# Layer 3 of a four-layer graph network: inverse sums kept on 32 partitions per head and spread by ScalarE copies, block sums in another pool, converted adjacency in a pool of its own

## The chip, the cores and the metric

The kernel runs on one core of one Trainium2 chip. TensorE (PE) multiplies matrices into PSUM, VectorE (DVE), ScalarE (ACT) and GpSimd (POOL) work element by element, and transfers are queued by SyncE (SP), ScalarE and GpSimd. The metric is the device time of one execution in microseconds; lower is better.

## The reference

A graph of 3,327 nodes with 256 features each, and a 3,327 x 3,327 adjacency. Four layers follow each other, each of them `x = layernorm(x + attention(x, adj))`. Layers 0 to 2 have one attention head. Layer 3 is two passes of a four-head attention (64 features per head), of which the first is what the change touches:

```python
h = jnp.einsum('nf,hfd->hnd', x, W)
f1 = jnp.einsum('hnd,hd->hn', h, a[:, :D])
f2 = jnp.einsum('hnd,hd->hn', h, a[:, D:])
e = jax.nn.leaky_relu(f1[:, :, None] + f2[:, None, :], ALPHA)
e = jnp.where(adj[None, :, :] > 0, e, NEG)
att = jax.nn.softmax(e, axis=-1)
out = jax.nn.elu(jnp.einsum('hnm,hmd->hnd', att, h))
```

The second pass takes the first one's output (nodes by 4 x 64 features) as its input, with other weights, and its result is added to x and normalised.

## The kernel before, in words

Nodes are cut into 26 tiles of 128 (the last has 127), and the tiles into four blocks of 7, 7, 6 and 6 (`blocks`, `sizes`), so a block has 896 or 768 columns. Layer 0 works with lists of neighbours and gathers (`sparse0`, L904, L924, L930, L1004, L1007) and takes the first half of the time. Layers 1 and 2 (`one_head`, L1688) and the two passes of layer 3, called l3a and l3b (`many_heads`, L1732), are dense: for each block b of target nodes they run over all 26 source tiles j.

In `many_heads`, one step j loads a tile of the adjacency as bf16 (`adjacent`, L1626; layer 1 loads it as int32, converts it on ScalarE and stores it for the later layers, L1635 to L1639). VectorE then makes four tiles of weights, one per head (`weigh`, L1614): `e = max(rate, q) * at`, in which the exponentials of the scores have been factored, so that no exponential is taken per edge. TensorE multiplies them in two column halves (`parts`): 16 matmuls of 32 feature columns (L1751) and 8 that sum the weights, each sum repeated on 32 partitions (L1759), so that partitions 32h to 32h+31 of `accs[x][pairs]` all hold the sum of head h. The accumulators fill six PSUM banks; two are left for everything else (`misc((6, 7))`).

At a block's end ScalarE copies the features (L1773, into `o`, features by nodes) and the sums (L1775, into `sums`) out of PSUM. What remains to be done with the block is a generator (`finish_hidden` for l3a, `finish_last` for l3b), appended to `pending`. `work_off` takes one step of it behind j = 0 and behind each j from 4 on of the next block (L1765), so that its instructions come into the engines' queues between those of the steps j. On PE, DVE and ACT the order is the program's (`manual_schedule`, L2004); on SP and POOL a scheduler sets it.

`finish_hidden` before: seven (or six) matmuls turn the sums to nodes by heads (`inverses`, L1794), VectorE takes the reciprocal of 28 or 24 numbers per partition (L1800), and then units of two node tiles go through the stages of `staged`: `spread` (eight matmuls with a broadcast inverse against the identity bring each head's inverses to its 64 feature partitions, L1833, and ScalarE copies them from PSUM, L1841), three steps later `scale` (VectorE multiplies `o`, L1846; ScalarE makes the exponential part of elu, L1810, L1811), then `elu` (L1852) and `project` (matmuls L1548 with the next pass's weights, and seven small ScalarE instructions per tile, L1557 to L1575). `staged` emits later stages first within a step. At the end the block's exponentials go through HBM to all partitions (`send_rates`, `load_rates`, L1594 to L1612).

Tiles of one tag in a pool share a fixed number of buffers. Tag "e" of the pool `edges` has 8: the weights, the int32 adjacency of layer 1, and the `sums` of layer 3. Tag "at" has 3. Tag "spread" of the pool `work` has 4.

Of the kernel before, what the change touches and what calls it, by code (L numbers as in the profile page):

```python
# [8 lines left out]
F32 = mybir.dt.float32  # L9
BF16 = mybir.dt.bfloat16  # L10
# [9 lines left out]
P = 128  # L20
BANK = 512
# [29 lines left out]
def gat_stack(  # L51
# [29 lines left out]
    nc = tc.nc  # L81
# [3 lines left out]
    heads = l3_w1.shape[0]  # L85
    hd = l3_w1.shape[2]
    assert dim == kc * P and heads * hd == dim

    def rows_of(it):
        return min(P, n - it * P)  # L90
# [4 lines left out]
    small = ctx.enter_context(tc.tile_pool(name="small", bufs=4))  # L95
# [124 lines left out]
    wide = max(sizes) * P  # L220
    banks_n = [(lo, min(n, lo + BANK)) for lo in range(0, n, BANK)]

    def cols_of(block):
        return block[0] * P, min(n, (block[-1] + 1) * P)
# [1273 lines left out]
    def layers(rs, early=0, rest=None):  # L1498


        head_p = rs.enter_context(tc.tile_pool(name="head_p", bufs=1))
        edges = rs.enter_context(tc.tile_pool(name="edges", bufs=3))
        work = rs.enter_context(tc.tile_pool(name="work", bufs=2))
        feats = rs.enter_context(tc.tile_pool(name="feats", bufs=1))
        rates = rs.enter_context(tc.tile_pool(name="rates", bufs=1))
# [10 lines left out]
        def misc(banks):  # L1516
            spare[0] += 1
            i = banks[spare[0] % len(banks)]
            return ps.tile([P, BANK], F32, tag=f"b{i}", name="misc")
# [106 lines left out]
        def adjacent(j, b, first=False):  # L1626

            pn = rows_of(j)
            c0, c1 = cols_of(blocks[b])
            w = c1 - c0  # L1630
            at = edges.tile([P, wide], BF16, tag="at", name="at")
            if not first:
                copy_rows(nc.sync, at[:pn, :w], at_d[j * P : j * P + pn, c0:c1])
                return at
            at_i = edges.tile([P, wide], I32, tag="e", name="at_i", bufs=8)  # L1635
            copy_rows(nc.sync, at_i[:pn, :w], adj_t[j * P : j * P + pn, c0:c1])
            nc.scalar.copy(at[:pn, :w], at_i[:pn, :w])  # L1637
            copy_rows(nc.scalar, at_d[j * P : j * P + pn, c0:c1], at[:pn, :w])
            return at_i  # L1639
# [92 lines left out]
        def many_heads(layer, nxt, finish):  # L1732

            pairs = layer.nh // 2
            for b, block in enumerate(blocks):
                c0, c1 = cols_of(block)
                half = (len(block) + 1) // 2 * P
                parts = [(0, half), (half, c1 - c0)]
                work_until(lambda: layer.rate[b] is not None)
                accs = [[bank(3 * x + y) for y in range(pairs + 1)] for x in range(len(parts))]  # L1740
                for j in range(nt):
                    pj = rows_of(j)
                    work_until(lambda: layer.feat[j] is not None)
                    at = adjacent(j, b)
                    es = [layer.weigh(j, b, at, h_of) for h_of in range(layer.nh)]
                    f = layer.feat[j]
                    for x, (lo, hi) in enumerate(parts):

                        for at0 in range(0, dim, 32):
                            p, q = divmod(at0, 2 * hd)  # L1750
                            nc.tensor.matmul(  # L1751
                                accs[x][p][q : q + 32, : hi - lo],
                                f[:pj, at0 : at0 + 32],
                                es[at0 // hd][:pj, lo:hi],
                                start=(j == 0), stop=(j == nt - 1),
                            )
                    for x, (lo, hi) in enumerate(parts):
                        for h_of in range(layer.nh):
                            nc.tensor.matmul(  # L1759
                                accs[x][pairs][h_of * 32 : (h_of + 1) * 32, : hi - lo],  # L1760
                                f[:pj, dim + h_of : dim + h_of + 1].to_broadcast([pj, 32]),
                                es[h_of][:pj, lo:hi],
                                start=(j == 0), stop=(j == nt - 1),
                            )
                    if j == 0 or j >= LATER:  # L1765
                        work_off()
                work_until(lambda: not pending)

                o = turn_p.tile([P, pairs, wide], F32, tag="ht", name="o")
                sums = edges.tile([P, wide], F32, tag="e", name="sums", bufs=8)  # L1770
                for x, (lo, hi) in enumerate(parts):
                    for p in range(pairs):
                        nc.scalar.copy(o[:, p, lo:hi], accs[x][p][:, : hi - lo])  # L1773
                for x, (lo, hi) in enumerate(parts):
                    nc.scalar.copy(sums[:, lo:hi], accs[x][pairs][:, : hi - lo])  # L1775
                pending.append(finish(b, o, sums))

        def staged(units, stages):

            last = max(at for _, at in units) + max(lag for lag, _ in stages)  # L1780
            for step in range(last + 1):
                for lag, what in reversed(stages):
                    for unit, at in units:
                        if at + lag == step:
                            what(unit)
                yield

        def inverses(block, sums, inv):

            full = [s for s, it in enumerate(block) if rows_of(it) == P]  # L1790
            turned = misc((6, 7))
            for s, it in enumerate(block):
                pn = rows_of(it)
                nc.tensor.matmul(  # L1794
                    turned[:pn, s * heads : (s + 1) * heads], sums[:, s * P : s * P + pn], heads_at,
                    start=True, stop=True,
                )
            yield
            w = len(full) * heads
            nc.vector.reciprocal(inv[:, :w], turned[:, :w])  # L1800
            if len(full) < len(block):
                pn = rows_of(block[-1])
                nc.vector.reciprocal(inv[:pn, w : w + heads], turned[:pn, w : w + heads])
            yield
# [7 lines left out]

        def finish_hidden(b, o, sums):
            block = blocks[b]
            inv = small.tile([P, max(sizes) * heads], F32, tag="invs", name="invs", bufs=2)
            yield from inverses(block, sums, inv)
            held = {}

            def cols(u):
                return u[0] * P, min((u[-1] + 1) * P, cols_of(block)[1] - cols_of(block)[0])  # L1820

            def spread(u):

                lo, hi = cols(u)
                m = misc((6, 7))
                m = m.rearrange("p (x i) -> p x i", x=heads // 2)
                for s in u:
                    pn = rows_of(block[s])
                    at0 = s * P - lo
                    for h_of in range(heads):  # L1830
                        p, q = divmod(h_of, 2)
                        k = s * heads + h_of
                        nc.tensor.matmul(  # L1833
                            m[q * hd : (q + 1) * hd, p, at0 : at0 + pn],
                            inv[:pn, k : k + 1].to_broadcast([pn, hd]),
                            ident[:pn, :pn], start=True, stop=True,
                        )
                t = held[u[0]] = work.tile(
                    [P, heads // 2, 2 * P], F32, tag="spread", name="spreads", bufs=4
                )  # L1840
                nc.scalar.copy(t[:, :, : hi - lo], m[:, :, : hi - lo])  # L1841

            def scale(u):
                lo, hi = cols(u)
                v, t = o[:, :, lo:hi], held[u[0]][:, :, : hi - lo]
                nc.vector.tensor_tensor(v, v, t, op=ALU.mult)  # L1846
                below(t, v)

            def elu(u):
                lo, hi = cols(u)  # L1850
                v, t = o[:, :, lo:hi], held.pop(u[0])[:, :, : hi - lo]
                nc.vector.scalar_tensor_tensor(v, t, -1.0, v, op0=ALU.add, op1=ALU.max)  # L1852

            def project(u):
                for s in u:
                    l3b.project(block[s], o[:, :, s * P : (s + 1) * P], (6, 7))

            units = [
                (tuple(range(s, min(s + 2, len(block)))), s) for s in range(0, len(block), 2)
            ]  # L1860
            yield from staged(units, [(0, spread), (3, scale), (6, elu), (7, project)])
            l3b.send_rates(b, (6, 7))
            yield
            yield
            l3b.load_rates(b)
            yield
# [229 lines left out]
```

## Time and profile before

| | us |
|---|---|
| median of 3 timed runs | 2984.57 (2984.07 to 2989.05) |
| profiled execution, its own time | 3407.64 |
| its span, first to last instruction | 3405.9 |
| TensorE busy | 2392.9 (70%) |
| VectorE busy | 2150.7 (63%) |
| ScalarE busy | 850.1 (25%) |
| GpSimd busy | 990.5 (29%) |
| weights of layers 1 and 3, L1620, of adjacency stored | 843.9, in 832 instructions |
| layer 3, features, L1751 | 690.4, in 6656 |
| layer 3, sums, L1759 | 376.0, in 3328 |
| layer 3, first pass, spread, L1833 (window of 2100 to 3406 us) | 14.0, in 200, and 0.6 in 8 |
| layer 3, both passes, turned sums, L1794 (the same window) | 12.5, in 100, and 0.7 in 4 |

A group's row gives the line, the engine, the operation, what it writes and reads, the shape and the count; then the busy time and the mean of one in ns; then the idle time of the engine just before, and what ended it. In the slices of the span a digit is the busy share in tenths. Rows of the timeline start with the start in us and the duration, and end with the idle time before them and its releaser in brackets. An fp32 matmul shows as two instructions. Layer 1 begins near 1790 us of the profile, layer 3 near 2400 us, its second pass near 2895 us.

### The profile page before, as it was taken

Reading aid. Unit: us, or ns where it says so; the run is one execution under the profiler, and the core shown is the slowest. Engines: PE = TensorE matmul, PEld = TensorE weight load, DVE = VectorE, ACT = ScalarE, POOL = GpSimd, SP = SyncE. Lnnn points to the kernel's source line nnn. Section 1 sums busy time; section 2 is a strip of 40 time slices with the busy share of each in tenths; the row PEclk is TensorE's granted clock in tenths of the full one; section 3 lists DMA queues with packets and bytes.
Section 4 is the critical chain, followed back from the end, with each engine's and each line's share of the span. In section 5 each row is a group of like instructions: output and inputs, shape, how many; then the busy total and the mean of one; then the engine's idle time right before and its main releaser. Section 6 shows DMA issues by size and latency. Waiting matters only on the chain. (4 is left out here: it accounts for less than half of the span.)

```text
span 3405.9 us, 45495 instructions
## 1 busy us (share of the span) xinstructions
PE 2392.9 (70%) x16122; PEld 1313.7 (39%) x16122; DVE 2150.7 (63%) x5633; ACT 850.1 (25%) x2372; POOL 990.5 (29%) x1061
## 2 busy tenths in 40 slices
PE   6155355543354533444368999999999999999997
PEld 4022122221121211122136888888443455344342
DVE  6268557565366654553463555310888989899997
ACT  3024233332242332323152343112011011110110
POOL 2723654655545656655620000000000000000000
PEclk8557667676676766677689999999999999999998
DMA  7454444433334333334317766333221222122111
GB/s 223 133 158 146 127 136 122 131 104 90 109 108 131 102 83 95 95 96 118 98 45 223 243 198 194 86 108 101 73 66 45 68 69 65 47 67 57 54 48 46
DMA packets 178607, 366.95 MB, mean 108 GB/s; under 512 B 34140, under 2 KB 119467, under 8 KB 177348
## 3 DMA queue, kind: packets, MB, share of 16 engines
q1 hardware_dynamic: 103994, 178.49, 18.4%
q0 software_dynamic: 51008, 155.70, 16.5%
q10 hardware_dynamic: 23370, 29.76, 2.5%
q8 instruction: 130, 2.13, 0.3%
q14 instruction: 105, 0.86, 0.1%
HBM read 324.06 MB, written 46.12 MB: 109 GB/s over the span
## 5 line engine op out<-in xcount | busy, mean ns | idle before, releaser
L904 POOL DMA_INDIRECT g<-table_d,lst x894 | 849.8, 951 | 383.0 <-issue 284.6
L1620 DVE SCALAR_TENSOR_TENSOR e<-rate,feat,at 128x896 f32<-128x896 f32 (+4 forms) x832 | 843.9, 1078 | 80.7 <-PE acc L1759 69.8
L1007 PE MATMUL acc<-g,ident 128*128 128x512 f32 (+1 forms) x896 | 547.9, 754 | 427.6 <-ACT g L1004 329.0
L1751 PE MATMUL acc<-e,feat 128*32 128x384 f32 (+2 forms) x6656 | 690.4, 516 | 7.5 <-DVE h L1724 4.7
L930 DVE SCALAR_TENSOR_TENSOR y<-y,a_ps 128x257 f32<-128x257 f32 x894 | 324.8, 418 | 243.1 <-remote 167.7
L1007 PEld LDWEIGHTS acc<-g,ident 128*128 128x128 f32 x896 | 204.5, 241 | 672.8 <-ACT g L1004 419.3
L1751 PEld LDWEIGHTS acc<-e,feat 128*32 128x32 f32 x6656 | 258.2, 110 | 348.7 <-issue 235.6
L1759 PE MATMUL acc<-e,feat 128*32 128x384 f32 (+3 forms) x3328 | 376.0, 512 | 0.0
L1004 ACT ACTIVATE g<-g,w 128x256 f32<-128x256 f32 x883 | 368.0, 495 | 23.9 <-issue 23.0
L1704 PE MATMUL acc<-feat,e 128*128 128x257 f32 (+2 forms) x1352 | 304.5, 382 | 13.6 <-DMA l2w<-in_l_w_dram 10.4
L924 DVE TENSOR_TENSOR y<-g,minus_ps 128x1028 f32<-128x1028 f32 (+2 forms) x233 | 272.9, 1171 | 23.9 <-issue 16.5
L1704 PEld LDWEIGHTS acc<-feat,e 128*128 128x128 f32 (+2 forms) x1352 | 255.6, 191 | 51.5 <-issue 11.4
L545 PE MATMUL v<-code,leads 65*128 65x512 bf16 (+1 forms) x182 | 85.9, 473 | 267.2 <-remote 71.1
L243 POOL TENSOR_TENSOR rstds<-rstds,minus_half 128x7 f32<-128x7 f32 (+1 forms) x12 | 19.7, 1641 | 776.0 <-DVE rstds L242 776.0
L1704 PE MATMUL acc<-feat,at 128*128 128x257 bf16 (+2 forms) x2028 | 237.5, 274 | 4.3 <-DMA at<-at_d 4.1
L571 DVE MAX8 cand<-v 128x8 f32<-128x104 f32 (+2 forms) x858 | 165.2, 260 | 111.3 <-issue 57.6
L1704 PEld LDWEIGHTS <-at 128*128 128x128 bf16 (+2 forms) x2028 | 198.5, 99 | 38.1 <-DMA at<-at_d 4.6
L1759 PEld LDWEIGHTS acc<-e,feat 128*32 128x32 f32 (+1 forms) x3328 | 138.9, 110 | 154.5 <-issue 130.9
L1620 DVE SCALAR_TENSOR_TENSOR e<-rate,feat,at_i 128x896 f32<-128x896 f32 (+2 forms) x104 | 111.5, 1080 | 72.3 <-DMA at_i<-in_adj_t_dram 58.5
L1600 POOL DMA_DIRECT2D rate3b_d<-rate_rows x4 | 2.1, 520 | 469.2 <-ACT rate_rows L1599 469.2
L545 PEld LDWEIGHTS <-leads 65*128 65x128 bf16 x182 | 22.4, 123 | 252.4 <-remote 75.6
L1637 ACT CAST at<-at_i 128x896 bf16<-128x896 int32 (+2 forms) x104 | 92.0, 885 | 103.6 <-DMA at_i<-in_adj_t_dram 84.2
(249 smaller groups left out, 1885.7 us busy)
## 6 DMA issues: line engine op xcount, KB each, us to landing
adj_i<-in_adj_dram SPq DMA_DIRECT2D x75, 512.0 KB
at<-at_d SPq DMA_DIRECT2D x150, 224.0 KB
at_i<-in_adj_t_dram SPq DMA_DIRECT2D x50, 448.0 KB
at<-at_d SPq DMA_DIRECT2D x75, 192.0 KB
at<-at_d SPq DMA_DIRECT2D x75, 191.8 KB
g<-table_d,lst POOLq DMA_INDIRECT x894
at_d<-at ACTq DMA_DIRECT2D x50, 224.0 KB
at_i<-in_adj_t_dram SPq DMA_DIRECT2D x25, 384.0 KB
```

What stands on the lines that cost most here:

```text
L545: nc.tensor.matmul(v[:, :w], leads[:, b, :], code[:, :w], start=True, stop=False)
L571: nc.vector.max(spread[:, c0 + c, :], view(v[:, :w]))
L904: nc.gpsimd.indirect_dma_start(out=g[:, k - k0, :], out_offset=None, in_=table_d[:, :], in_offset=bass.IndirectOffsetOnAxis(ap=entry["lst" ...
L924: nc.vector.tensor_tensor(y, rows, minus_src[:, None, :].to_broadcast([P, m, dim + 1]), op=ALU.max)
L930: nc.vector.scalar_tensor_tensor(y, y, 1.0, a_ps[:, : dim + 1], op0=ALU.mult, op1=ALU.mult, accum_out=sc)
L1004: nc.scalar.activation(rows, rows, AF.Copy, scale=w[:, k : k + 1])
L1007: nc.tensor.matmul(dst, ident, rows, start=start, stop=stop)
L1620: nc.vector.scalar_tensor_tensor(e[:pn, : c1 - c0], self.rate[b][:pn, h_of, : c1 - c0], q, at[:pn, : c1 - c0], op0=ALU.max, op1=ALU.mult,)
L1637: nc.scalar.copy(at[:pn, :w], at_i[:pn, :w])
L1704: nc.tensor.matmul(accs[s][:pn, : dim + 1], a[:pj, s * P : s * P + pn], f[:pj, : dim + 1], start=(j == 0 and part == 0), stop=(j == nt - 1 ...
L1751: nc.tensor.matmul(accs[x][p][q : q + 32, : hi - lo], f[:pj, at0 : at0 + 32], es[at0 // hd][:pj, lo:hi], start=(j == 0), stop=(j == nt - 1),)
L1759: nc.tensor.matmul(accs[x][pairs][h_of * 32 : (h_of + 1) * 32, : hi - lo], f[:pj, dim + h_of : dim + h_of + 1].to_broadcast([pj, 32]), es[ ...
```

## The change

In `finish_hidden` the sums stay where they are, repeated on 32 partitions per head. VectorE takes their reciprocal in place, over whole halves of a block (512 and 384, or 384 and 384, columns). `spread` no longer uses TensorE: eight ScalarE copies per unit, each of 32 partitions, bring the inverses to the 64 partitions of each head. Units don't cross the halves, so a block of six tiles has units of 2, 1, 2 and 1 tiles; they start two steps apart; `scale` comes one step after `spread`, `elu` three and `project` four. The sums of both passes become two tiles of the tag "spread" instead of one of tag "e". The converted adjacency moves from `edges` to a pool `links`, which lies behind it.

```diff
-        edges = rs.enter_context(tc.tile_pool(name="edges", bufs=3))
+        edges = rs.enter_context(tc.tile_pool(name="edges", bufs=8))
+        links = rs.enter_context(tc.tile_pool(name="links", bufs=3))
...
-            at = edges.tile([P, wide], BF16, tag="at", name="at")
+            at = links.tile([P, wide], BF16, tag="at", name="at")
...
-                sums = edges.tile([P, wide], F32, tag="e", name="sums", bufs=8)
+                sums = [
+                    work.tile([P, BANK], F32, tag="spread", name="sums", bufs=4) for _ in parts
+                ]
...
-                    nc.scalar.copy(sums[:, lo:hi], accs[x][pairs][:, : hi - lo])
+                    nc.scalar.copy(sums[x][:, : hi - lo], accs[x][pairs][:, : hi - lo])
...
+                x, at0 = divmod(s, (len(block) + 1) // 2)
                 nc.tensor.matmul(
-                    turned[:pn, s * heads : (s + 1) * heads], sums[:, s * P : s * P + pn], heads_at,
-                    start=True, stop=True,
+                    turned[:pn, s * heads : (s + 1) * heads],
+                    sums[x][:, at0 * P : at0 * P + pn], heads_at, start=True, stop=True,
                 )
...
-            inv = small.tile([P, max(sizes) * heads], F32, tag="invs", name="invs", bufs=2)
-            yield from inverses(block, sums, inv)
+            total = cols_of(block)[1] - cols_of(block)[0]
+            half = (len(block) + 1) // 2
             held = {}
 
+            for x, t in enumerate(sums):
+                w = min(half * P, total - x * half * P)
+                nc.vector.reciprocal(t[:, :w], t[:, :w])
+            yield
...
             def spread(u):
 
                 lo, hi = cols(u)
-                m = misc((6, 7))
-                m = m.rearrange("p (x i) -> p x i", x=heads // 2)
-                for s in u:
-                    pn = rows_of(block[s])
-                    at0 = s * P - lo
-                    for h_of in range(heads):
-                        p, q = divmod(h_of, 2)
-                        k = s * heads + h_of
-                        nc.tensor.matmul(
-                            m[q * hd : (q + 1) * hd, p, at0 : at0 + pn],
-                            inv[:pn, k : k + 1].to_broadcast([pn, hd]),
-                            ident[:pn, :pn], start=True, stop=True,
-                        )
+                x, at0 = divmod(u[0], half)
+                at0 *= P
                 t = held[u[0]] = work.tile(
                     [P, heads // 2, 2 * P], F32, tag="spread", name="spreads", bufs=4
                 )
-                nc.scalar.copy(t[:, :, : hi - lo], m[:, :, : hi - lo])
+                for h_of in range(heads):
+                    p, q = divmod(h_of, 2)
+                    for to in range(q * hd, (q + 1) * hd, 32):
+                        nc.scalar.copy(
+                            t[to : to + 32, p, : hi - lo],
+                            sums[x][h_of * 32 : (h_of + 1) * 32, at0 : at0 + hi - lo],
+                        )
...
-            units = [
-                (tuple(range(s, min(s + 2, len(block)))), s) for s in range(0, len(block), 2)
-            ]
-            yield from staged(units, [(0, spread), (3, scale), (6, elu), (7, project)])
+            units, at = [], 1
+            for x in range(0, len(block), half):
+                for s in range(x, min(x + half, len(block)), 2):
+                    u = tuple(range(s, min(s + 2, x + half, len(block))))
+                    units.append((u, at))
+                    at += 2
+            yield from staged(units, [(0, spread), (1, scale), (3, elu), (4, project)])
```

More of the change, by code (lines that the diff above doesn't have):

```diff
@@ L1814, in finish_hidden @@
             block = blocks[b]
-            inv = small.tile([P, max(sizes) * heads], F32, tag="invs", name="invs", bufs=2)
-            yield from inverses(block, sums, inv)
+            total = cols_of(block)[1] - cols_of(block)[0]
+            half = (len(block) + 1) // 2
             held = {}
+            for x, t in enumerate(sums):
+                w = min(half * P, total - x * half * P)
+                nc.vector.reciprocal(t[:, :w], t[:, :w])
+            yield
             def cols(u):
-                return u[0] * P, min((u[-1] + 1) * P, cols_of(block)[1] - cols_of(block)[0])
+                return u[0] * P, min((u[-1] + 1) * P, total)
             def spread(u):
                 lo, hi = cols(u)
-                m = misc((6, 7))
-                m = m.rearrange("p (x i) -> p x i", x=heads // 2)
-                for s in u:
-                    pn = rows_of(block[s])
-                    at0 = s * P - lo
-                    for h_of in range(heads):
-                        p, q = divmod(h_of, 2)
-                        k = s * heads + h_of
-                        nc.tensor.matmul(
-                            m[q * hd : (q + 1) * hd, p, at0 : at0 + pn],
-                            inv[:pn, k : k + 1].to_broadcast([pn, hd]),
-                            ident[:pn, :pn], start=True, stop=True,
-                        )
+                x, at0 = divmod(u[0], half)
+                at0 *= P
                 t = held[u[0]] = work.tile(
```

## The prediction

> **What bounds it now.** First the page (slices and groups), then busy time by window (engine busy times in the order PE, PEld, DVE, ACT, POOL, then granted clock and DMA share), then TensorE's and VectorE's order in time where one row block of layer 3 meets the next, then ScalarE's groups.
>
> ```profile
> PE  6155355543354533444368999999999999999997
> ...
> DVE  6268557565366654553463555310888989899997
> ...
> L1620 DVE SCALAR_TENSOR_TENSOR e<-rate,feat,at 128x896 f32<-128x896 f32 (+4 forms) x832 | 843.9, 1078 | 80.7 <-PE acc L1759 69.8
> ...
> 2650.00:2900.00 250.00, 250.00 (x2918) 129.73 (x2910) 225.19 (x244) 35.98 (x132) 2.13 (x4) 1.00 0.21 61
> ```
>
> The changed lines run in layer 3, the last third. From 2650 to 2900 us TensorE is busy for 250.0 of 250 us, VectorE for 225, ScalarE for 36. TensorE bounds, VectorE is close behind, and its waits are for the weighted-sum matmuls (L1759) to give back weight buffers. One node tile j of an 896-wide block costs TensorE 4.51 us and VectorE 4.26 (four weights); 768 wide, 3.87 and 3.78.
>
> The end of the first block, TensorE and then VectorE:
>
> ```profile
> 2535.59 3.36 PE L1751 MATMUL acc<-e,feat 128*32 128x512 f32 x28
> ...
> 2540.96 1.73 PE L1794 MATMUL misc<-heads_at,sums 128*128 128x4 f32 x14
> ...
> 2565.30 1.09 PE L1833 MATMUL misc<-ident,invs 128*64 128x128 f32 x16
> ...
> 2601.08 2.05 PE L1548 MATMUL misc<-l3bw,o 128*128 128x264 f32 x8
> ...
> 2551.86 4.34 DVE L1620 SCALAR_TENSOR_TENSOR e<-rate,feat,at 128x896 f32<-128x896 f32 x4 [0.17 <-PE acc L1759]
> 2556.12 0.32 DVE L1800 RECIPROCAL invs<-misc 128x28 f32<-128x28 f32 x1
> 2556.37 4.34 DVE L1620 SCALAR_TENSOR_TENSOR e<-rate,feat,at 128x896 f32<-128x896 f32 x4
> ```
>
> VectorE waits 0.17 us per j: with eight buffers, weights for j+2 start when j is done and end as j+1 does. Head 3's weight is first wanted 1.28 us into a j (6 of its 24 matmuls; 0.21 us each at 512 columns), so VectorE may be some 1.25 us late before TensorE stops.
>
> ScalarE, by shape and in time:
>
> ```profile
> L1004 ACT ACTIVATE g<-g,w 128x256 f32<-128x256 f32 x883 | 368.0, 495 | 23.9 <-issue 23.0 <-DMA g<-table_d,lst 0.9
> ...
> 1004.72 4.88 ACT L1004 ACTIVATE g<-g,w 128x256 f32<-128x256 f32 x12
> ...
> 2602.27 0.17 ACT L1557 ACTIVATE feat<-misc 128x4 f32<-128x4 f32 x1 [5.35 <-PE misc L1548]
> ...
> 2604.43 0.66 ACT L1810 ACTIVATE spreads<-o 128x512 f32<-128x512 f32 x1
> ```
>
> Twelve 256-column instructions in a row took 4.88 us: 0.40 us each. The projection that began at 2601.08 held ScalarE until 2604.43, 3.43 us after TensorE had finished its j at 2601.0.
>
> [...] The trace: 128x20, 24, 28 took 280, 301, 323 ns, 5.4 ns per element[...]. [...] 0.40 was measured on 128 partitions, none here on 32. [...] here 4.65 us of idle before 2399.98 left 0.50 in 2400 to 2404.
>
> **The change, part by part.**
> *Removed from TensorE (layer 3's first pass, l3a).* L1794: 1.65 us per block end. L1833: 1.03 us per pair of tiles (j periods of 5.54 instead of 4.51), 3.6 us for seven tiles, 3.1 for six; four finishes: 13.4 us. The four block ends cost 2.51, 2.59, 2.37, 2.30 us over a plain j (7.02, 6.46, 6.24 and 6.81 from the first j's start to the second's): 9.8 in all, L1794 plus about 0.5 from the sums holding one of the eight buffers, so that head 3's weight comes late.
>
> *Added to VectorE.* Two reciprocals over 512+384 or 384+384 columns, behind the four weights of the next block's first j and ahead of those of its second. No row shows this width. At 5.4 ns per element with 0.1 us of start: 4.9 us for seven tiles, 4.2 for six. [...] I take the measured slope. Block end at T0 = 2535.59: the sums' copy is there at T0+0.44, reciprocals until 5.4, four weights until 9.7, then 18 of the 24 matmuls are left, 3.2 us: second j done at 12.9, before 11.56. That is +1.35; likewise +1.7, +1.25, +0.9 at the others: +5.2. With the 13.4 saved: -8.2 us. [...]
>
> *Added to ScalarE, and a shorter lag.* The spread is eight copies of 32 partitions per unit, 3.3 us with latency (128 columns: 0.11 less each by the 512- and 384-column copies, 2.35). Its product on VectorE (scale) comes one step later, not three. For units 0 and 1 nothing is ahead on ScalarE and the copies end in time. From unit 2, the step that spreads a unit also projects an earlier one, and the changed program puts the projection's evictions first in ScalarE's queue. With E the end of that step's matmuls (j = 9): evictions until E+3.43, copies until E+6.7, scale (0.6) until E+7.4. VectorE had finished the weights of j = 10 near E and waits. Behind scale stand the weights of j = 11, done at E+11.7; TensorE needs another 3.2: E+14.9. Undisturbed it is the projection 2.05 and two j's, E+11.07. Stall: 3.85 us. Unit 3 alike, with one tile: 2.65 (projection until 3.43, copies 5.8, scale 6.3, weights 10.5, j done 13.7 against 11.07). At width 768, with 3.78 and 2.9 for 4.26 and 3.2, 4.3 and 3.2. With a single tile projected before unit 3 (six tiles) 3.0 at 768, 2.55 at 896. Over the four finishes: 6.5+7.5+7.3+6.4 = 27.7 us. At no cost of the copies it would still be 27.7-4x3.3-4x2.35 = 5; at 0.5 us per copy, 34.
>
> *Layer 3's second pass.* It keeps L1794 and small reciprocals, with the sums out of the ring: 3 block ends by 0.5: -1.5. If the ring isn't what delays there, 0.
>
> *Layer 1.* Weight buffers now begin the region, the converted adjacency comes behind. In the changed order the first adjacency load moves ahead of the late feature stores on SP, behind the three feature loads of 1567 us (0.33 us of issue, in a queue that then waits for stores until 1573), and its weight into VectorE's 29.4 us wait after 1554.4, so it is hidden by that wait (a load slower than 12 us would delay layer 0 by the rest). All later adjacency loads are one tile earlier against the bias and weight loads. TensorE became continuous at its third j (1809.28) with 3.07 us per j; it now should be a j further: -3.1, between 0 and -5.
>
> *Nothing:* buffer counts are as before; the sums take two of four spread buffers, but the product tile of unit 2 takes that of the finished first half; the conversion's ScalarE work is unmoved; rates of the next pass come three steps earlier, and POOL waited for them 469 us with nobody waiting behind.
>
> Sum: -8.2+27.7-1.5-3.1 = +14.9 us, on the profiled execution's 3407.64 us (span 3405.9). The timed runs' median is 2984.57, so the profile stretches something; the terms lie in stages at full clock, and I carry them over in microseconds: 2999.5, say 2999.
>
> **Rivals.**
> 1. *The new wait is hidden, faster.* If VectorE's weights stood further ahead of TensorE, only the removed work would tell: -12.8, 2972 us. It decides where the lead covers the stall of about 4 us, besides today's; the buffer waits of 0.17 us show 1.25. For it: VectorE's idle of 1.3 to 2 us around projections. 0.08.
> 2. [...] 0.24.
> 3. [...] -8.2+5-4.6 = -8, 2977 with free copies. 0.11.
> 4. *The change in layer 1 holds VectorE in layer 0* behind a late load: some 10 us more, 3010. Against it: 29 us of cover. 0.03.
>
> Likeliest, the sum as worked: 0.54. Its own range is 2990 to 3006 (copies at 0.30 to 0.45 us, slope 5 to 6.5). Over all cases 8 in 10 lie in 2983 to 3015. About 0.2%, 6 us, is what a measurement can tell from no change. Slower: the likeliest but for its lowest edge (0.53), 2 and 4 give 0.80; same: 3 and that edge, 0.12; faster: 1, 0.08.
>
> **What would show it.** In the profile after: RECIPROCAL sums 128x512 near 2.9 us; VectorE waits of about 5 to 7 us before L1846's counterpart for units 2 and 3, released by ScalarE's spread copies, eight in all; weight loads of TensorE waiting for L1620's counterpart; TensorE's first j's of a block without L1794; first layer-1 weight near 1575 us. Wrong if ScalarE runs the spread ahead of the evictions, if the reciprocal's rate is elsewhere than 5 to 6 ns, or if VectorE's wait falls where TensorE waits for something else.

## The result, and the profile after

The changed kernel takes 3009.7 us (median of 5 runs, 3000.35 to 3010.3) where the kernel before takes 2984.57 (5 runs, 2983.09 to 2989.05): ratio 1.0083, 95% interval 1.0071 to 1.0096, 25.1 us slower. The forecast was 2999 and slower, so the sign was right and 10.7 us were missing.

In some sessions, that of the forecast's profile among them, layer 0 took some 420 us longer for every kernel, the kernel before included (why is open; one chip showed both), while the later layers took the same, so ratios are taken within a session and layer 3 is compared across them. The place to compare is therefore layer 3 from its first matmul to the end: 1005.8 us before, 1032.8 after. These 27.0 us hold the whole loss.

First the page (slices, one group):

```profile
PE   6566657556545415568999999999999999999997
...
DVE  6889799968875347764555321178888989899997
...
L1621 DVE SCALAR_TENSOR_TENSOR e<-rate,feat,at 128x896 f32<-128x896 f32 (+4 forms) x832 | 841.2, 1079 | 47.3 <-PE acc L1760 36.3
```

Then 250 us around the start of the third row block, as shown of the kernel before (PE, PEld, DVE, ACT and POOL busy, granted clock, DMA share):

```profile
2232.00:2482.00 250.00, 237.27 (x2612) 137.20 (x2608) 220.35 (x234) 52.81 (x185) 2.13 (x4) 0.99 0.20 57
```

The slices hardly show it: nines before and after. The window does. TensorE, which was busy for 250.0 of 250 us, is now busy for 237.3. VectorE waits less for TensorE to give buffers back (36.3 us, 69.8 before): it is no longer ahead. (All 832 weights of that row are layer 3's: 26 j's, four heads, eight blocks.)

The first block end, TensorE and then VectorE, in time:

```profile
2110.66 3.36 PE L1752 MATMUL acc<-e,feat 128*32 128x512 f32 x32
...
2117.86 4.88 PE L1752 MATMUL acc<-e,feat 128*32 128x512 f32 x28 [2.34 <-DVE e L1621]
...
2111.07 5.76 DVE L1825 RECIPROCAL sums<-sums 128x512 f32<-128x512 f32 x2 [0.20 <-ACT sums L1778]
2116.75 25.49 DVE L1621 SCALAR_TENSOR_TENSOR e<-rate,feat,at 128x896 f32<-128x896 f32 x24
```

The two reciprocals take 5.8 us, and TensorE stands idle for 2.34 us before the second j's first matmul. After them 24 weights follow without a gap: VectorE is catching up.

Then the steps of units 2 and 3 of the same finish, on ScalarE, VectorE and TensorE:

```profile
2164.20 0.19 ACT L1576 ACTIVATE columns<-misc 128x4 f32<-128x4 f32 x1
2164.25 3.28 ACT L1842 COPY spreads<-sums 32x256 f32<-32x256 f32 x8
...
2160.97 0.68 DVE L1856 SCALAR_TENSOR_TENSOR o<-spreads,o 128x512 f32<-128x512 f32 x1
2167.57 0.69 DVE L1850 TENSOR_TENSOR o<-o,spreads 128x512 f32<-128x512 f32 x1 [5.92 <-ACT spreads L1842]
2168.18 8.58 DVE L1621 SCALAR_TENSOR_TENSOR e<-rate,feat,at 128x896 f32<-128x896 f32 x8
...
2182.87 0.43 DVE L1850 TENSOR_TENSOR o<-o,spreads 128x256 f32<-128x256 f32 x1 [5.50 <-ACT spreads L1842]
...
2160.90 2.05 PE L1549 MATMUL misc<-l3bw,o 128*128 128x264 f32 x8
2169.38 5.93 PE L1752 MATMUL acc<-e,feat 128*32 128x512 f32 x30 [1.78 <-DVE e L1621]
2177.06 2.05 PE L1549 MATMUL misc<-l3bw,o 128*128 128x264 f32 x8
2184.41 4.89 PE L1752 MATMUL acc<-e,feat 128*32 128x512 f32 x28 [0.65 <-DVE e L1621]
```

This is the chain that the forecast drew. The projection starts at 2160.90; its evictions (seven small ScalarE instructions per tile that take its result out of PSUM) hold ScalarE until 2164.25, the eight copies until 2167.5; VectorE, done with the weights at 2161, stands before the scale for 5.92 us, and only then makes the weights that TensorE wants. The totals, from the list of waits (us, times, longest):

```profile
PEld acc L1752 <- DVE e L1621: 117.0, 169, 3.5
...
DVE o L1850 <- ACT spreads L1842: 42.0, 8, 6.4
```

In the kernel before, TensorE's weight loads waited for VectorE for half as long:

```profile
PEld acc L1751 <- DVE e L1620: 62.4, 137, 2.9
```

**Where the 27 us lie.** The first matmul of each j gives its period. Per finish (what `finish_hidden` does with one block, during the next one), the sum of the periods of its 26 j's was 131.61, 115.05, 112.75 and 129.43 us, and is 138.09, 122.51, 120.76 and 135.82: +28.4 in all.

For the parts, the end of a j's last sum is the better mark, because neighbouring j's overlap on TensorE. Undisturbed, the next j's first matmul begins 0.2 us before the last sum ends. After the late weights of a block end it begins 0.6 to 1.0 us before, j after j, until a projection comes, which follows the last sum. The tenth j of the first finish, TensorE:

```profile
2155.45 0.60 PE L1752 MATMUL acc<-e,feat 128*32 128x512 f32 x2
...
2155.97 0.49 PE L1760 MATMUL acc<-e,feat 128*32 128x384 f32 x2
...
2159.30 1.67 PE L1760 MATMUL acc<-e,feat 128*32 128x512 f32 x12
2160.90 2.05 PE L1549 MATMUL misc<-l3bw,o 128*128 128x264 f32 x8
```

Its first matmul begins at 2155.45, before the ninth j's last sum ends at 2156.46, and its own last sum ends at 2160.97: 5.5 us, where an undisturbed j takes 4.7; the period is 4.51 in both cases. So first matmuls show only at the projection (a period of 7.43 us for 6.60) a part of what was lost at the block end. By step, counted to the ends of the last sums where nothing else is said, summed over the four finishes (a plain j is 4.51 us at 896 columns, 3.87 at 768):

| step | forecast | measured | how |
|---|---|---|---|
| block ends (first five j's) | +5.2 | +10.9 | 4.86, 5.56, 5.27 and 4.41 over plain j's for 2.37, 2.46, 2.22 and 2.15 |
| spread on TensorE removed | -13.4 | -15.3 | periods: 4.18, 4.18, 3.48 and 3.47 over plain j's, now nothing |
| stalls in the steps of units 2 and 3 | +27.7 | +31.5 | from the eleventh j on 60.8 over plain j's, for 29.3 in the run without these waits (below, the spread issued first) |
| not in the forecast | 0 | +1.3 | sixth to tenth j 0.7; four projections for three in the two blocks of six tiles, 0.3 each |
| second pass, sums out of the ring | -1.5 | -1.35 | from 381.38 to 380.03 us after the last finish |
| layers 0 to 2 | -3.1 | -1.9 | 25.1 less 27.0 |
| sum | +14.9 | +25.1 | |

### The profile page after: what moved, and what is told of

The parts are those of the page before. It is cut to its first block, busy times and chain, and to the rows that moved or that the text cites. A ratio compares the mean times of both kernels' runs of the same rounds, so it can differ in the third digit from the quotient of the medians.

```text
span 3007.9 us, 45092 instructions
## 1 busy us (share of the span) xinstructions
PE 2349.5 (78%) x15841; PEld 1335.4 (44%) x15862; DVE 2159.5 (72%) x5640; ACT 886.3 (29%) x2490; POOL 992.4 (33%) x1061
## 5 line engine op out<-in xcount | busy, mean ns | idle before, releaser
L1621 DVE SCALAR_TENSOR_TENSOR e<-rate,feat,at 128x896 f32<-128x896 f32 (+4 forms) x832 | 841.2, 1079 | 47.3 <-PE acc L1760 36.3
L1752 PE MATMUL acc<-e,feat 128*32 128x384 f32 (+2 forms) x6656 | 736.7, 518 | 29.0 <-DVE e L1621 21.6
L1007 PE MATMUL acc<-g,ident 128*128 128x512 f32 (+1 forms) x896 | 510.5, 714 | 260.4 <-ACT g L1004 237.5
L1752 PEld LDWEIGHTS acc<-e,feat 128*32 128x32 f32 x6656 | 290.1, 110 | 375.6 <-issue 174.1
L1007 PEld LDWEIGHTS acc<-g,ident 128*128 128x128 f32 x896 | 196.8, 230 | 479.5 <-ACT g L1004 359.4
L1760 PE MATMUL acc<-e,feat 128*32 128x384 f32 (+3 forms) x3328 | 403.8, 512 | 0.0
L1760 PEld LDWEIGHTS acc<-e,feat 128*32 128x32 f32 (+1 forms) x3328 | 156.0, 110 | 133.9 <-issue 95.1
L571 DVE MAX8 cand<-v 128x8 f32<-128x104 f32 (+2 forms) x858 | 158.6, 259 | 18.6 <-PE v L548 18.6
L1776 ACT COPY o<-acc 128x384 f32<-128x384 f32 (+2 forms) x32 | 16.2, 507 | 342.3 <-PE acc L1752 342.1
```

Source lines behind the costliest of these rows:

```text
L571: nc.vector.max(spread[:, c0 + c, :], view(v[:, :w]))
L1007: nc.tensor.matmul(dst, ident, rows, start=start, stop=stop)
L1621: nc.vector.scalar_tensor_tensor(e[:pn, : c1 - c0], self.rate[b][:pn, h_of, : c1 - c0], q, at[:pn, : c1 - c0], op0=ALU.max, op1=ALU.mult,)
L1752: nc.tensor.matmul(accs[x][p][q : q + 32, : hi - lo], f[:pj, at0 : at0 + 32], es[at0 // hd][:pj, lo:hi], start=(j == 0), stop=(j == nt - 1),)
L1760: nc.tensor.matmul(accs[x][pairs][h_of * 32 : (h_of + 1) * 32, : hi - lo], f[:pj, dim + h_of : dim + h_of + 1].to_broadcast([pj, 32]), es[ ...
```

## The experiments

**Order and lag on ScalarE.** Theory A is the forecast's chain. Theory B puts the stalls down to the reciprocals, which use up VectorE's lead, theory C to the copies' length in any order. Two edits take the wait away in different ways, and two make one of its parts small. For all four the kernel before took 2983.0 us.

```diff
-            yield from staged(units, [(0, spread), (1, scale), (3, elu), (4, project)])
+            yield from staged(units, [(1, scale), (3, elu), (4, project), (0, spread)])
```

> The changed kernel, but each step issues the spread copies ahead of the projection (and with it of its evictions on ScalarE). Before layer 3's end the changed kernel loses, per finish, about 9 us in the steps of units 2 and 3. Theory A (the spread copies stand behind the projection's evictions in ScalarE's order, VectorE stands in order behind the scale that waits for them): the eight waits of 5 to 6 us at the scale vanish, of the 35 us of stalls about 6 are left, the time falls by 25 to 30 us to 2980-2985. Theory B (the two wide reciprocals have used up VectorE's lead over TensorE, so that any later VectorE work stops TensorE whatever it waits for): at most 15 us come back, 2995 or more. Theory C (the copies themselves are too long, in any order): under 5 us come back, 3005 or more.

2977.06 us, ratio to before 0.9978 (0.9970 to 0.9986), 32.6 us less than the changed kernel and somewhat under the 2980 to 2985 of theory A. The four finishes fell from 517.2 to 485.4 us; every other part of layer 3 was the same within 0.1 us. The same step on VectorE, and ScalarE behind the evictions:

```profile
2161.74 0.68 DVE L1856 SCALAR_TENSOR_TENSOR o<-spreads,o 128x512 f32<-128x512 f32 x1
2162.34 0.69 DVE L1850 TENSOR_TENSOR o<-o,spreads 128x512 f32<-128x512 f32 x1
2162.95 4.33 DVE L1621 SCALAR_TENSOR_TENSOR e<-rate,feat,at 128x896 f32<-128x896 f32 x4
...
2164.99 0.19 ACT L1576 ACTIVATE columns<-misc 128x4 f32<-128x4 f32 x1
2165.04 0.66 ACT L1814 ACTIVATE spreads<-o 128x512 f32<-128x512 f32 x1
...
2166.27 2.43 ACT L1842 COPY spreads<-sums 32x128 f32<-32x128 f32 x8
```

The scale follows elu with no wait, because its copies were done before; the evictions come later, and nothing waits for them. None of the 16 scales waits for a copy. The same instructions with the same durations, in another order, are worth 32 us: A, and neither B nor C. This alone makes the change 6 us faster than the kernel before.

```diff
-            yield from staged(units, [(0, spread), (1, scale), (3, elu), (4, project)])
+            yield from staged(units, [(0, spread), (3, scale), (6, elu), (7, project)])
```

> The changed kernel with the lags of the kernel before (scale three steps behind spread, elu six, project seven), so that no step both spreads and projects. Theory A (order on ScalarE together with the short lag): no wait of VectorE for the copies, 25 to 30 us less than the changed kernel, 2980-2985, the same as with the spread issued first. Theory B (VectorE's lead is used up): at most 15 us less, 2995 or more. Theory C (copies too long): with three steps between, about 13 us each, the copies are covered too, so as A; C would be told from A by the run with the spread issued first.

2976.45 us, ratio 0.9980 (0.9973 to 0.9987), finishes 483.8 us. The lag does the same as the order; what the wait needs is both, the short lag and the projection's evictions ahead.

```diff
-                for h_of in range(heads):
-                    p, q = divmod(h_of, 2)
-                    for to in range(q * hd, (q + 1) * hd, 32):
-                        nc.scalar.copy(
-                            t[to : to + 32, p, : hi - lo],
-                            sums[x][h_of * 32 : (h_of + 1) * 32, at0 : at0 + hi - lo],
-                        )
+                for p in range(heads // 2):
+                    nc.scalar.copy(t[:, p, : hi - lo], sums[x][:, at0 : at0 + hi - lo])
```

> The changed kernel with two spread copies of 128 partitions per unit in place of eight of 32 (the values are then those of other heads, the work behind is the same): 0.8 us instead of 3.3 per unit, 0.6 instead of 2.4 for a single tile. Theory A: the scale of units 2 and 3 still waits for the evictions, about 3.4 us, but 2.5 and 1.8 us less than now; of the 35 us of stalls 12 to 15 are left[...]: 2987-2992. Theory B (VectorE's lead): within 8 us of the changed kernel. Evictions alone as the cause (copies of no account): within 5 us of it.

2989.69 us, ratio 1.0020 (1.0013 to 1.0027), finishes 498.4: 18.8 of the 35 us come back. The eight waits at the scale fell from 42.0 to 23.4 us, by 2.3 us each, as the copies became 2.5 or 1.8 us shorter:

```profile
DVE o L1845 <- ACT spreads L1840: 23.4, 8, 3.9
```

What is left of the wait is the evictions ahead and the rest of the copies.

```diff
-                nc.vector.reciprocal(t[:, :w], t[:, :w])
+                nc.vector.reciprocal(t[:, : w // 8], t[:, : w // 8])
...
-                        nc.scalar.copy(
+                        nc.scalar.activation(
                             t[to : to + 32, p, : hi - lo],
-                            sums[x][h_of * 32 : (h_of + 1) * 32, at0 : at0 + hi - lo],
+                            sums[x][h_of * 32 : (h_of + 1) * 32, at0 : at0 + hi - lo], AF.Copy,
+                            scale=1e-9,
                         )
```

> The changed kernel with reciprocals over an eighth of the columns (64 and 48) in the finish of the first pass, the rest left as sums, and the spread copies scaled by 1e-9 so that nothing overflows: it leaves 7/8 of the reciprocals' time out, about 5 us per finish. Theory A: the block ends of the four finishes come to some 10 us less than before the change instead of 8 more: 18 us less; the eight waits at the scale stay, 5 to 6 us each, and with them about 32 of the 35 us: 2988-2993. Theory B (the stalls of units 2 and 3 come from the lead that the reciprocals use up): the stalls go too, 40 us or more less, 2970 or less.

2993.93 us, ratio 1.0030 (1.0017 to 1.0043), finishes 499.5: 17.7 us less than in the changed kernel. VectorE in time at the first block end:

```profile
2113.15 1.07 DVE L1825 RECIPROCAL sums<-sums 128x64 f32<-128x64 f32 x2 [0.19 <-ACT sums L1778]
2114.14 16.99 DVE L1621 SCALAR_TENSOR_TENSOR e<-rate,feat,at 128x896 f32<-128x896 f32 x16
```

And from the list of waits:

```profile
DVE o L1851 <- ACT spreads L1842: 42.0, 8, 6.2
```

The block ends are all but gone (1.4 us over plain j's at the four together, 20.1 in the changed kernel), and the eight waits are what they were, 42.0 us. So two causes stand beside each other, and B isn't the stalls' cause: the wide reciprocals cost some 19 us at the block ends (18.2 if counted by first matmuls), the copies' place in the order 32.

**Scale on another engine.**

```diff
-                nc.vector.tensor_tensor(v, v, t, op=ALU.mult)
+                nc.gpsimd.tensor_tensor(v, v, t, op=ALU.mult)
```

> The changed kernel with only the engine of the scale changed: GpSimd multiplies the features by the spread inverses, VectorE no longer stands behind the copies; order, lag and copies are as changed. Theory A (the loss is VectorE standing in order behind the copies): no wait of VectorE for spreads, 30 us or more of the 35 come back, 2975-2980, although the copies end as late as in the changed kernel. Theory C (the inverses come too late for TensorE itself): 3000 or more. Third case: GpSimd takes over 4 us for 128x512, or VectorE's weights grow longer than 1.08 us beside it, then 2980-3000.

Ratio to before 1.0006 (0.9987 to 1.0025), where the kernel before took 3423.3 us; layer 3 took 1007.4 us, 25.5 less than in the changed kernel. GpSimd now does the waiting, and VectorE goes on. But not for free; VectorE and GpSimd in one of these steps:

```profile
2608.98 5.41 DVE L1621 SCALAR_TENSOR_TENSOR e<-rate,feat,at 128x896 f32<-128x896 f32 x4 [2.45 <-PE acc L1760]
...
2608.97 1.28 POOL L1850 TENSOR_TENSOR o<-o,spreads 128x512 f32<-128x512 f32 x1 [43.05 <-ACT spreads L1842]
```

Four weights, 4.33 us elsewhere, took 5.41 where they began together with GpSimd's multiply: 1.08 us of VectorE's time beside 1.28 of GpSimd's. Why isn't shown. The first scales of a finish fall behind the reciprocals, where VectorE has no lead, and there the first four periods lost 6.5 us more than in the changed kernel (7.03 and 5.28 for 6.02 and 4.51 in the first finish; how much of the 6.5 is GpSimd's doing isn't shown). So some 32 us of stalls came back and 6.5 were given away: between A and the third case.

**Ring and pools, each by itself.** The sums of the kernel before as two tiles of another tag, with the lines that use them, nothing else:

```diff
-                sums = edges.tile([P, wide], F32, tag="e", name="sums", bufs=8)
+                sums = [
+                    work.tile([P, BANK], F32, tag="spread", name="sums", bufs=4) for _ in parts
+                ]
...
```

> The kernel before with the block sums outside the ring of weights (two tiles of the tag of the spread buffers) and nothing else. The forecast's step says 0.5 us at each of seven block ends: 3.5 us less than before, about 2979.5, and layer 3 from its first matmul to its end 1002.3 us for 1005.8. Rival, from the run with short reciprocals (block ends without any loss, where the kernel before lost 2.3 to 2.6 us, of which the turned sums took 1.65 to 1.73): 0.75 us each, 5 us less, 2978. Ring of no account: 2983.

Layer 3 took 1002.0 us, 3.8 less than before, for 3.5 forecast. The four first-pass block ends fell by 0.58, 0.66, 0.66 and 0.58 us, as the forecast's step has it. In the second pass only the first block end did (0.58); the other two fell by 0.07 each, and another 0.34 came in a later step of the last block and 0.34 after its last j. The ratio, 1.0006 (0.9987 to 1.0026), can't show as little (3423.4 us for 3423.3).

```diff
-        edges = rs.enter_context(tc.tile_pool(name="edges", bufs=8))
-        links = rs.enter_context(tc.tile_pool(name="links", bufs=3))
+        edges = rs.enter_context(tc.tile_pool(name="edges", bufs=3))
...
-            at = links.tile([P, wide], BF16, tag="at", name="at")
+            at = edges.tile([P, wide], BF16, tag="at", name="at")
```

> The changed kernel with the converted adjacency back in the pool of the weights, as before the change; the rest is the changed kernel's. Theory A (layers 0 to 2 as forecast: the earlier adjacency load brings layer 1 about 3 us): 3 us more than the changed kernel, 3010-3013. Rival (what layer 1's start gains, the start of the third row block of layer 2 loses again, 3.1 us in the profile of the changed kernel, and the first weight of layer 1 that VectorE works on 13 us late in layer 0 is covered): within 1.5 us of the changed kernel, layer 3 the same 1032.8 us from its first matmul to the end. Second rival (that 13 us wait is not covered): 8 us or more below the changed kernel, 3000 or less.

Ratio 1.0086 (1.0058 to 1.0114), layer 3 at 1032.0 us. The times (3452.5 us for 3423.3) were too uneven to show a few microseconds; a second measurement has the changed kernel beside it.

> The changed kernel itself, once more, to stand beside the next one on the same chip. 0.8 to 0.9% more than the kernel before.

> The changed kernel with the converted adjacency back in the pool of the weights, a second time, since layer 0 ran 430 us slower and less evenly on the chip of the first time, which hid a few microseconds. Theory A (3 us gained in layer 1): 3 us over the changed kernel beside it. Rival (gained at layer 1's start, lost at layer 2's third row block): within 1.5 us.

3005.85 us (3002.27 to 3011.5) for the changed kernel, 3010.7 (3002.77 to 3013.99) with the pools back; ratios to before 1.0083 (1.0069 to 1.0096) and 1.0092 (1.0077 to 1.0108). The intervals overlap: not told apart. In the traces, layer 1's fourth j begins 21.9 to 23.7 us after layer 0's last gather matmul in the nine profiles with the new pool, 23.3 to 24.4 in the five without: about 1 us. The first weight of layer 1 does hold VectorE in layer 0, behind the reciprocal of L1031 (changed kernel, VectorE):

```profile
1176.44 0.15 DVE L1031 RECIPROCAL inv<-total 128x1 f32<-128x1 f32 x1
1189.97 1.15 DVE L1621 SCALAR_TENSOR_TENSOR e<-rate,feat,at_i 128x896 f32<-128x896 f32 x1 [13.38 <-issue]
```

Yet layer 0's last gather matmul begins at 1360.6 and 1360.0 us with it and at 1362.3 without: the 13 us are covered. Layer 2 took 265.7 to 271.8 us with the new pool, 267.6 to 271.0 without, so the late start of its third row block in the profile after (3.1 us) is not the change's.

**A better order for the reciprocals.** They become a stage of their own, one unit at a time:

```diff
-            for x, t in enumerate(sums):
-                w = min(half * P, total - x * half * P)
-                nc.vector.reciprocal(t[:, :w], t[:, :w])
-            yield
+            def recip(u):
+                lo, hi = cols(u)
+                x, at0 = divmod(u[0], half)
+                t = sums[x][:, at0 * P : at0 * P + hi - lo]
+                nc.vector.reciprocal(t, t)
...
-            units, at = [], 1
+            units, at = [], 0
...
-                    at += 2
-            yield from staged(units, [(0, spread), (1, scale), (3, elu), (4, project)])
+                    at += 3
+            yield from staged(units, [(0, recip), (1, spread), (4, scale), (5, elu), (6, project)])
```

> The changed kernel with the reciprocal as a stage of its own, 256 or 128 columns per unit, units three steps apart, and the spread one step after it, scale four, elu five, project six, so that VectorE gets one extra instruction of at most 1.7 us per step and no step both spreads and projects. With the stalls gone (31.7 to 33.4 us in the two runs that removed them) what is left are the block ends, which lose 18.2 us to the wide reciprocals. If VectorE's lead of about 1.25 us and its 0.25 us per step (0.09 at 768) are what a reciprocal has to fit into, most of that comes back: 1.5 us or less per block end is lost, and 2 to 3 us per finish in the 768-wide blocks where VectorE's sum is as long as TensorE's: 2964-2970. If total work on VectorE is the bound rather than its order: 2974-2978, no better than the longer lag alone.

Ratio to before 0.9944 (0.9915 to 0.9972), 3402.4 us for 3423.3; layer 3 988.1 us. A second time, beside the changed kernel above:

> The version with the reciprocals by unit, a second time, for a closer ratio: layer 3 was 988.1 us from its first matmul to its end, 17.7 less than in the kernel before and 12.9 less than with the spread issued first, so 2965 where the kernel before takes 2983, ratio 0.994.

2962.9 us (2960.85 to 2965.32) where the kernel before takes 2982.26 and the changed kernel 3005.85: ratio to before 0.9938 (0.9924 to 0.9952). It beats both. VectorE at the first block end:

```profile
2106.46 1.75 DVE L1830 RECIPROCAL sums<-sums 128x256 f32<-128x256 f32 x1 [0.20 <-ACT sums L1778]
2108.13 25.49 DVE L1621 SCALAR_TENSOR_TENSOR e<-rate,feat,at 128x896 f32<-128x896 f32 x24
```

The window of 250 us, with the columns of above:

```profile
2232.00:2482.00 250.00, 249.32 (x2860) 126.44 (x2856) 242.18 (x260) 56.47 (x196) 2.13 (x4) 1.00 0.22 62
```

VectorE is busy for 242 us of this window, 220 in the changed kernel's, and TensorE for 249.3: total work is not the bound, its order is. By the ends of the last sums, the four block ends now cost 0.85 to 1.2 us each over plain j's, with 1.75 us of reciprocal, where the whole reciprocals at once (5.8 us at the first) cost 4.4 to 5.6.

**The profile of before once more.**

> The kernel before itself, for a second profile: the one that the forecast read was taken in an execution of 3407.64 us, 423 us over the median. If the forecast's carrying over of microseconds was sound, those 423 us lie in layer 0, and layer 3 takes 1005.8 us from its first matmul to the end in this profile too. If the stretch was spread over the layers, layer 3 is shorter here, and part of the 27 us between the two profiles' layer 3 was not the change's.

A single execution, 3401.91 us: layer 3 takes 1005.9 us again, the four finishes agree with the forecast's profile to 0.01 us each, and layer 1's fourth j begins at 1803 us where it begins at 1383 in the changed kernel's profile. So layer 0 was long again, and the 27 us of layer 3 are the change's. There is no profile of the kernel before with a short layer 0, so layer 0 is compared by medians and by the kernel with the pools back.

## Why the prediction was right or wrong

- **What bounds the kernel**: right. TensorE bounds layer 3, and VectorE's lead decides what is felt. At the first block end the lead was less than the 1.25 us forecast: reciprocals of 1.07, 1.75 and 5.76 us cost 0.17, 0.85 and 4.86 us there (one eighth, one unit, the whole), each 0.9 us less than its length.
- **The shorter lag** (+27.7): the mechanism was right in each link: the eight waits (42.0 us, 5.25 each, for 5 to 7 forecast), the evictions ahead (3.35 us for 3.43), the copies (401 and 293 ns for 0.40 and 0.29). The size was short by 3.8 us, in the last step: "another 3.2" us from the weights' end to TensorE's took about 3.9 even at full clock. For unit 3 eight weights begin at 2183.21 and take 8.58 us, so four end near 2187.5, and the next projection begins at 2191.37. That is about 0.5 us in each of the first finish's two stalls and 3.1 us over all eight; a spell of half clock in the profile after (last section) makes up the other 0.7. Why the step takes 3.9 us isn't shown.
- **Left out of the sum** (+1.3): one step before these stalls, elu and the next scale follow each other on VectorE, 1.3 us, and in the two 768-wide blocks, where its weights take nearly as long as TensorE's j, that cost 0.7 us together. With the lag put back they don't share a step, and 0.2 us is left; with the scale on GpSimd VectorE has only elu there, and nothing is. The 0.3 us for each block of six tiles comes from its units of 2, 1, 2 and 1 tiles, which make four projections in place of three.
- **The reciprocals**: the slope of 5.4 ns, taken from 20 to 28 elements, was too low. Two rows of the groups (busy us, mean ns):

```profile
L1825 DVE RECIPROCAL sums<-sums 128x384 f32<-128x384 f32 x5 | 12.5, 2516 | 0.0
...
L1825 DVE RECIPROCAL sums<-sums 128x512 f32<-128x512 f32 x2 | 6.7, 3353 | 0.9 <-ACT sums L1778 0.9
```

  (3353 - 2516) / 128 is 6.5 ns per element, so 5.9 us per seven tiles for 4.9. The block ends cost +10.9 for +5.2; in the second profile of the changed kernel, where the granted clock was 1.00 on average from 2100 to 2480 us (0.99 in the profile after, where two block ends had a spell at 0.50), +9.5. Beside the slope it is the same last step: at the first block end the four weights end near 2121.0 and the second j's last sum at 2124.9, again 3.9 us for 3.2. That the slope up to 28 columns holds up to 512 was the author's estimate. Rival 2, a slower reciprocal, rested on nothing that a trace of this case showed.
- **Removed from TensorE** (-13.4): 15.3, since the j that held a pair's spread took 5.65 us and not the 5.54 that the forecast read (1.14 over a plain j for 1.03), and that with a single tile 5.21 (0.7 for 0.5).
- **The second pass** (-1.5): 1.35, with luck. Only one of its three block ends gained as forecast (0.58 us); the other two gained 0.07 each, and 0.7 came elsewhere in the last block, in the changed kernel as in the run with the ring alone. Why is open.
- **Layer 1** (-3.1): mis-sized. The start came forward by about 1 us; the medians less layer 3 put layers 0 to 2 between -2.1 and +1.7 us against before over the seven runs with the new pool and a short layer 0. A first load that comes early is of little use while the next ones are late: in the profile after, VectorE waits 6.5, 6.1 and 3.0 us for the adjacency of the second to fourth weight. Rival 4, that the early weight holds layer 0, had its wait (13.4 us) and not its effect.
- **Rivals 1 and 3**: neither. No wait was hidden (42.0 us in eight), and the copies were not cheap (401 and 293 ns each). That the 2977 us of rival 3 for free copies is what two other orders reached, with copies of the same length, is chance.
- **Carrying microseconds over** from a profile 423 us above the median: sound, as the 423 us lay in layer 0.

The range of 2983 to 3015 held the time. The likeliest case's own range, 2990 to 3006, didn't: the copies were within its bounds and the slope at their edge, and what was not in it is the longer last step of block ends and stalls, the terms left out and the spells of half clock.

## What to carry to other kernels

In a kernel whose engines run their instructions in order, a short wait costs what is queued behind it (here eight waits of 5.25 us, 32 us with what stood behind them): before shortening the distance between a producer and its consumer, look at what else the producer's engine has queued in the same step, and issue what others wait for first. An engine that is only a microsecond ahead of the bound can take long instructions if they come in pieces near that lead, far enough apart for it to be won back (1.75 us cost 0.85 at the first block end, 5.76 us cost 4.86). Two causes of like size, a long instruction and a wait in order, are told apart by removing each alone. And where an engine's steps overlap, a loss can surface in a later step than the one that caused it: mark the ends of steps as well as their starts.

## What the runs showed of the hardware

- The reciprocal on VectorE took 0.95 and 1.74 us for 128 and 256 fp32 columns in SBUF (reciprocals by unit), 2.52 and 3.35 for 384 and 512 (changed kernel): 6.0 to 6.5 ns per further column, against 5.4 for 20 to 28 columns from PSUM.
- ScalarE copies of 32 partitions took 401 ns for 256 columns and 293 for 128; the exponential part of elu (L1814), 256 columns on 128 partitions, took 417 in the same profile.
- Four VectorE weights that began together with a GpSimd multiply of 1.28 us took 5.41 us for 4.33. In the first finish 32 weights beside GpSimd's multiplies of 2.15 and 1.73 us took 36.23 us, where 24 took 25.49 in the changed kernel, or 34.0 for 32: 2.2 us more. With the features and inverses 512 wide GpSimd took 1.28 to 2.15 us for the multiply, VectorE 0.69.
- TensorE's granted clock was at half after some short stops and full after others. In the changed kernel, after the stop before 2169.38 (windows, columns as above):

```profile
2170.00:2172.00 2.00, 1.99 (x8) 0.33 (x8) 2.00 (x3) 0.00 (x0) 0.00 (x0) 0.66 0.00 0
2172.00:2174.00 2.00, 2.00 (x14) 0.70 (x12) 2.00 (x3) 0.00 (x0) 0.00 (x0) 0.50 0.25 41
```

  The stop was 1.78 us by the records and followed by matmuls that came one weight at a time, at 0.66 and 0.50; the period was 9.66 us. In the second profile the stop at the same place was 1.77 us, the period 8.94, and the 28 matmuls behind it took 4.89 us, as those at 1.00 do in the profile after (2184.41). The profile after has eight stops of 1.77 to 2.84 us in its four finishes: those of 1.78, 2.84 and 1.94 us were followed by stretches at 0.50, those of 2.34, 2.28, 2.29, 1.89 and 1.77 us by 1.00. What decides it isn't shown.
